# Full-width one-hots in place of column tiles in the first level of an edge sum

## The chip, the cores and the metric

The kernel runs on one core of a Trainium2 chip. The metric is the device time of one execution in microseconds; nine runs of the kernel before are given by their median. TensorE (PE) multiplies matrices, VectorE (DVE), ScalarE (ACT) and GpSimd (POOL) work on tiles in SBUF and PSUM, SyncE (SP) issues transfers. Each engine takes its instructions in a fixed order, and waits between engines are semaphores.

## What is computed

A graph with 12,500 nodes of 64 features and 400,000 edges, sorted by destination, passes two layers.

```python
def _L0_gnn_ref(x, edge_attr, ...):
    x_t = _mlp2(x, W1n, b1n, W2n, b2n)
    e_t = _mlp2(edge_attr, W1e, b1e, W2e, b2e)
    msgs = x_t[src] * e_t * dp_scale
    aggregated = jax.ops.segment_sum(msgs, dst, num_segments=num_nodes)
    out = x + aggregated * res_w
    ...                       # layernorm with gamma, beta
def _L1_gnn_ref(x, edge_index, W, b):
    ...                       # K = 2 hops: h = segment_sum(edge_weight * h[col], row)
    return h @ W.T + b
x = _layernorm(x + _L0_gnn_ref(x, ...))
x = _layernorm(x + _L1_gnn_ref(x, ...))
```

The change touches the `segment_sum` of the first layer: sums of message rows over edges with the same destination.

## The kernel before

A step `q` of 261 handles 12 chunks (`QC`) of 128 edges. Four consecutive superchunks of three chunks (`SCC`) make a step, and the destinations of a superchunk lie within 32 consecutive nodes (`REL`). Steps run from the last edge to the first, and a step is spread over four passes of the main loop, so that four steps are in flight:

- `hidden` (L624 to L638): the first layer of the edge network, two f32 matmuls on row tiles, then ACT and DVE.
- `message` (L648 to L659), in two halves: second layer on PE, and on DVE the product with the gathered rows `xg`, into one of three message tiles `msg` of 65 columns (the last is 1, for the degree).
- `level1` (L674 to L693): DVE builds the one-hot `oh` (128 edges x 12 chunks x 32 columns) of each edge's node within its superchunk's 32. PE multiplies each chunk's one-hot (128x32, the stationary side) with its messages (128x65) and adds the three chunks of superchunk `s` into partitions 32`s` to 32`s`+31 of a PSUM bank `pl`; each superchunk has its own column tile of PE. ACT copies the bank to `tot` (L693). The 128 rows of `tot` are sums for the four windows of 32 nodes.
- `level2` (L703, L713): a second one-hot puts these rows into their window of 128 nodes in a PSUM `ring`; it runs one pass later.

GpSimd gathers the rows `xg` (L592), 12 indirect transfers a step, paced by marks on PE's matmuls. When a group of nodes is complete, `nodes` normalises it.

Between these units the main loop interleaves two generators: `adjacency` (L859 to L944), which builds a dense table of edge counts from one-hots on DVE (L910, a pool `ohp` of 11 buffers), matmuls (L920) and copies on ACT (L935), and `hop1` (L1097 to L1251), which multiplies the table with node features (L1117, L1129), copies the result (L1169) and turns it (L1246, f32, 128x128 weights, 64 columns). From about 5780 us only the second hop and the output remain (L1221, L1232, L1479, L1594).

A scheduler with a model of engine times puts the instructions into each engine's order; the units of the main loop have high priority. A tile in a pool with n buffers can be written again when the n-th last use has ended. The one-hot `oh` of level 1 lives in `edgep` with two buffers; PSUM has seven banks for all users beside the ring.

Of the kernel before, what the change touches and what calls it, by code (L numbers as in the profile page):

```python
# [11 lines left out]
F32 = mybir.dt.float32  # L12
# [9 lines left out]
P = 128  # L22
# [10 lines left out]
SCC = 3  # L33
QC = 4 * SCC
# [6 lines left out]
REL = 32  # L41
# [157 lines left out]
def tile_fast(  # L199
# [42 lines left out]
    nc = tc.nc  # L242
# [34 lines left out]
    with tc.tile_pool(name="srch", bufs=2) as srch, tc.tile_pool(  # L277
        name="srch1", bufs=1
# [125 lines left out]
        iota_f = const.tile([P, 4 * P], F32, name="iota_f")  # L404
# [51 lines left out]
        with tc.tile_pool(name="tmp1", bufs=1) as t1:  # L456
            r = t1.tile([1, D], F32, name="b2r")
            nc.sync.dma_start(r, b2e[None, :])
            for k in range(3):
                h = t1.tile([1, D], BF16, name=f"b2h{k}")  # L460
                nc.vector.tensor_copy(h, r)
                if k < 2:
                    r2 = t1.tile([1, D], F32, name=f"b2r{k}")
                    nc.vector.tensor_sub(r2, r, h)
                    r = r2
# [46 lines left out]

    edgep = main.enter_context(tc.tile_pool(name="edgep", bufs=2))
    msgp = main.enter_context(tc.tile_pool(name="msgp", bufs=1))
    hopp = main.enter_context(tc.tile_pool(name="hopp", bufs=3))
    hevp = main.enter_context(tc.tile_pool(name="hevp", bufs=2))
    lnp = main.enter_context(tc.tile_pool(name="lnp", bufs=1))
    counts = ExitStack()
    slotp = counts.enter_context(tc.tile_pool(name="slotp", bufs=1))
    slotq = counts.enter_context(tc.tile_pool(name="slotq", bufs=2))  # L520
    ohp = counts.enter_context(tc.tile_pool(name="ohp", bufs=11))
    kohp = counts.enter_context(tc.tile_pool(name="kohp", bufs=10))
    stgp = counts.enter_context(tc.tile_pool(name="stgp", bufs=3))
    psR = main.enter_context(tc.tile_pool(name="psR", bufs=1, space=PSUM))
# [2 lines left out]
    def bank(shape, name):  # L527

        n = math.prod(shape[1:])
        t = banks.tile([P, 512], F32, name=name, tag="bank")[:, :n]  # L530
        if len(shape) == 3:
            t = t.rearrange("p (a b) -> p a b", b=shape[2])
        elif len(shape) == 4:
            t = t.rearrange("p (a b c) -> p a b c", b=shape[2], c=shape[3])
        return t
# [4 lines left out]
    for i in range(3):  # L540
        m = msgp.tile([P, QC, D + 1], F32, name=f"msg{i}")
# [127 lines left out]
    def level1(q):  # L669
        def f():  # L670
            _, rel = seg[q // SEGQ]
            c0 = (q % SEGQ) * QC
            oh = edgep.tile([P, QC, REL], F32, name="oh1")
            nc.vector.tensor_tensor(  # L674
                oh,
                iota_f[:, None, :REL].to_broadcast([P, QC, REL]),
                rel[:, c0 : c0 + QC, None].to_broadcast([P, QC, REL]),
                op=ALU.is_equal,
            )
            pl = bank([P, D + 1], "pl")  # L680
            m = msgs[q % 3]
            for s in range(4):
                for c in range(SCC):
                    nc.tensor.matmul(  # L684
                        pl[REL * s : REL * (s + 1), :],
                        oh[:, s * SCC + c, :],
                        m[:, s * SCC + c, :],
                        start=(c == 0),
                        stop=(c == SCC - 1),
                        tile_position=(0, REL * s),  # L690
                    )
            tot = edgep.tile([P, D + 1], F32, name="tot")
            nc.scalar.copy(tot, pl)  # L693
            tots[q] = tot

        return f
# [634 lines left out]
    for t in range(NQ + 3):  # L1331
# [23 lines left out]
        for u in range(parts * len(units)):  # L1355
# [5 lines left out]
            while a_live and a_spent < a_goal:  # L1361
                c = next(a_gen, None)
# [5 lines left out]
            while h_live and h_budget > 0:  # L1368
                try:
                    c = next(h_gen)  # L1370
# [301 lines left out]
    for c in range(NSC):  # L1672
        if c + 1 < NSC:
            tiles[c + 1] = [load_dense(*d, c + 1) for d in dense]
        w = min(SC, PITCH - c * SC)
# [45 lines left out]
        for j in range(max(0, min(-(-w // P), W0 - wi0))):  # L1721
            m = min(P, w - j * P)
# [5 lines left out]
                start=False,  # L1728
                stop=False,
                skip_group_check=True,  # L1730
            )
        for j in range(max(0, min(-(-w // P), W0 - wi0))):
            m = min(P, w - j * P)
# [5 lines left out]
                start=False,  # L1739
                stop=False,  # L1740
                skip_group_check=True,
                tile_position=(0, D * h),
# [572 lines left out]
def build(nc, fast, general, params, out, **kw):  # L2315
    with tile.TileContext(nc, schedule_with_timeline_sim=True) as tc, ExitStack() as ctx:
        fp = ctx.enter_context(tc.tile_pool(name="flag", bufs=1))
        flag = fp.tile([1, 1], I32, name="flag")
        tile_fast(tc, flag, *fast, *params, out, **kw)
        again = nc.values_load(flag, min_val=0, max_val=1)  # L2320
        with tc.If(again > 0):
            tile_general(
                tc, *general, *params, out.rearrange("(p j) d -> p j d", j=NJ)
            )
# [27 lines left out]
```

## Time and profile before

| quantity | value |
|---|---|
| median of 9 runs | 6575.74 us (6550.13 to 6584.31) |
| the profiled execution, its own time | 6566.46 us |
| its span from first to last instruction | 6564.7 us |
| mean granted PE clock, share of full | 0.801 |
| PE busy | 5072.8 us, 77% of the span |
| GpSimd busy | 3744.3 us, 57% |
| DVE busy | 3321.8 us, 51% |
| ACT busy | 2272.1 us, 35% |
| level 1's one-hots on DVE (L674) | 261, 145.7 us, 558 ns each |
| level 1's copies on ACT (L693) | 261, 56.2 us, 215 ns each |

The profile is of one execution. Busy time counts instructions, not waits. The end of a matmul is modelled, so a matmul record tells when it was started and not surely when its result was there. An f32 matmul leaves two records. The granted clock of PE switches between 1.0 and 0.5. A wait is put down to the instruction whose semaphore ended it; "remote" or "unknown queue" stands where no instruction's end fits, and "issue" where the profile shows no wait.

### The profile page before, as it was taken

The numbers are of one execution on the slowest core, as the hardware profiler recorded it, in microseconds if no ns is written. First come the engines' busy times: TensorE is split into PE (matmuls) and PEld (weight loads), VectorE is DVE, ScalarE is ACT, GpSimd is POOL, SyncE is SP. The second block draws the span as 40 slices with busy tenths as digits, with TensorE's granted clock in tenths as the row PEclk, the third lists the DMA queues.
The fourth block names the chain that finished last, engine by engine and source line by source line (L and its number), as shares of the span: only waits on it lengthen the run. The fifth ranks groups of instructions, "written<-read, shape, count | busy, mean of one in ns | idle before, by whom it ended". The sixth has DMA issues, their size and how long they took to land. (4 is left out here: it accounts for less than half of the span.)

```text
span 6564.7 us, 94126 instructions
## 1 busy us (share of the span) xinstructions
PE 5072.8 (77%) x31344; PEld 2865.0 (44%) x31344; DVE 3321.8 (51%) x11086; ACT 2272.1 (35%) x7868; POOL 3744.3 (57%) x3607
## 2 busy tenths in 40 slices
PE   4666788888888788876777678867866786589998
PEld 2333344544444444443444444434434443344444
DVE  5667565555455555555555555555656664330003
ACT  2667565444333333333333333223322111220002
POOL 5666455556555555555444555555665553448886
PEclk6777788888887787777777678878877786599999
DMA  3655454544444354423333243323322223269998
GB/s 105 144 128 120 108 124 111 113 112 108 102 106 100 76 114 99 96 62 85 87 92 89 55 101 88 87 53 91 88 56 58 56 55 98 75 166 212 210 201 216
DMA packets 1254835, 696.95 MB, mean 106 GB/s; under 512 B 593468, under 2 KB 1188144, under 8 KB 1253312
## 3 DMA queue, kind: packets, MB, share of 16 engines
q1 hardware_dynamic: 1104032, 566.91, 34.0%
q0 software_dynamic: 150304, 123.92, 11.2%
q8 instruction: 248, 4.06, 0.3%
q14 instruction: 251, 2.06, 0.1%
HBM read 494.67 MB, written 195.83 MB: 105 GB/s over the span
## 5 line engine op out<-in xcount | busy, mean ns | idle before, releaser
L592 POOL DMA_INDIRECT xg<-xt_tab,si x3125 | 3080.8, 986 | 2549.8 <-PE pa L920 768.0
L935 ACT ACTIVATE stage<-pa 128x391 fp8e4<-128x391 f32 x3077 | 1507.6, 513 | 1563.5 <-PE pa L920 1109.4
L910 DVE TENSOR_SCALAR oh<-iota_b,colT 128x391 bf16<-128x391 bf16 x5556 | 1620.6, 333 | 737.9 <-PE pa L920 466.3
L920 PE MATMUL pa<-oh,koh 128*128 128x391 bf16 (+2 forms) x6054 | 1412.6, 406 | 276.5 <-issue 135.7
L920 PEld LDWEIGHTS <-koh 128*128 128x128 bf16 (+2 forms) x6054 | 627.6, 154 | 780.3 <-issue 526.8
L1117 PE MATMUL hacc_p<-at,gp 128*128 128x512 fp8e4 (+1 forms) x2425 | 768.4, 454 | 87.3 <-DMA at<-adj 38.0
L624 PE MATMUL pw<-eat,w1ab 64*128 64x384 f32 x1044 | 511.0, 763 | 285.3 <-ACT tot L693 209.5
L935 ACT ACTIVATION_READ_ACCUMULATOR stage<-pa 128x1 f32 x3077 | 673.4, 219 | 0.0
L674 DVE TENSOR_TENSOR oh<-iota_f,rel 128x384 f32<-128x384 f32 x261 | 145.7, 558 | 999.1 <-remote 739.9
L713 PE MATMUL ring<-tot,oh 128*128 128x65 f32 x1096 | 260.1, 384 | 405.0 <-ACT tot L693 340.6
L1492 POOL DMA_INDIRECT hop_tab<-tot,first x317 | 493.7, 1558 | 101.0 <-issue 95.7
L650 PEld LDWEIGHTS pe<-w,z 128*128 128x128 f32 x3132 | 475.1, 213 | 106.9 <-issue 86.2
L650 PE MATMUL pe<-w,z 128*128 128x128 f32 x3132 | 485.5, 296 | 0.0
L1117 PEld LDWEIGHTS <-gp 128*128 128x128 bf16 x2425 | 262.6, 115 | 477.0 <-issue 289.3
L713 PEld LDWEIGHTS ring<-tot,oh 128*128 128x128 f32 x1096 | 220.9, 283 | 556.4 <-ACT tot L693 389.9
L693 ACT COPY tot<-pl 128x65 f32<-128x65 f32 x261 | 56.2, 215 | 1145.4 <-remote 794.0
L659 DVE TENSOR_TENSOR msg<-pe,xg 128x384 f32<-128x384 f32 x522 | 288.0, 552 | 322.0 <-PE pe L650 245.6
L1221 PE MATMUL acc<-at,gp 128*128 128x512 fp8e4 (+1 forms) x2000 | 446.3, 376 | 0.0
L1129 PE MATMUL hacc_p<-at,gp 128*64 128x512 fp8e4 (+1 forms) x2425 | 386.9, 401 | 11.9 <-issue 11.3
L859 DVE TENSOR_TENSOR koh<-iota_k,keyT 128x512 bf16<-128x512 bf16 (+3 forms) x920 | 384.9, 420 | 0.0
L634 ACT ACTIVATE z<-pw,b1s 128x384 f32<-128x384 f32 x522 | 290.9, 599 | 215.4 <-PE pw L624 105.7
L1246 PEld LDWEIGHTS pc<-twoid,hev 128*128 128x128 f32 x1764 | 332.5, 274 | 75.2 <-issue 40.7
(218 smaller groups left out, 4381.1 us busy)
## 6 DMA issues: line engine op xcount, KB each, us to landing
adj<-stage SPq DMA_DIRECT2D x390, 391.0 KB
at<-adj SPq DMA_DIRECT2D x97, 896.0 KB
at<-adj SPq DMA_DIRECT2D x168, 512.0 KB
eat<-in_eaq_dram SPq DMA_DIRECT2D x261, 192.0 KB
xg<-xt_tab,si POOLq DMA_INDIRECT x3125
at<-adj SPq DMA_DIRECT2D x96, 256.0 KB
at<-adj SPq DMA_DIRECT2D x24, 832.0 KB
at<-adj SPq DMA_DIRECT2D x24, 768.0 KB
```

Of the source, the lines that this page charges most:

```text
L592: got = nc.gpsimd.indirect_dma_start(out=xg[:, i, :], out_offset=None, in_=xt_tab, in_offset=bass.IndirectOffsetOnAxis(ap=si[:, c : c + 1] ...
L624: nc.tensor.matmul(pws[h], w1ab[rows, h, :], ea_q[rows], start=True, stop=True, tile_position=(D * h, 0),)
L650: ended = nc.tensor.matmul(pe[:, :, c, :], z[:, h, c * P : (c + 1) * P], w2, start=False, stop=(c == SCC - 1),)
L713: nc.tensor.matmul(ring[:, w % RING, :], oh[:, (w - lo) * P : (w - lo + 1) * P], tot, start=False, stop=False, skip_group_check=True,)
L859: nc.vector.tensor_tensor(t[:, :, :n], iota_8[:, :, :n] if w == 8 else iota_k[:, : w * FA, :n], keyT[:, None, j0 : j0 + n].to_broadcast([P ...
L910: nc.vector.tensor_scalar(oh, iota_b, colT[:, i % P : i % P + 1], None, op0=ALU.is_equal)
L920: ended = nc.tensor.matmul(to, key, oh, start=(j == 0), stop=(j == caps[g] - 1), tile_position=(0, r0),)
L935: nc.scalar.activation(stage[:, u, :], pa, AF.Identity, saturate=True, accum_out=sums[:, u : u + 1],)
L1117: nc.tensor.matmul(acc[:, :w], gp[:kk, lo + i, 0:2, :].rearrange("p t d -> p (t d)"), t[:kk, i, :w], start=start, stop=False, skip_group_c ...
L1129: nc.tensor.matmul(acc[D * h : D * (h + 1), :w], gp[:kk, lo + i, 2, :], t[:kk, i, :w], start=False, stop=False, skip_group_check=True, til ...
L1221: nc.tensor.matmul(acc[:, :w], gp[:kk, wi, 0:2, :].rearrange("p t d -> p (t d)"), t[:kk, wi - lo, :w], start=first and n == 0, stop=False, ...
L1492: nc.gpsimd.indirect_dma_start(out=hop_tab[(q * QC + i) % HT], out_offset=bass.IndirectOffsetOnAxis(ap=first[:, q - Q0, i : i + 1], axis=0 ...
```

## The change

Level 1's one-hot of a chunk becomes 128 columns wide. Only the 32 columns of its superchunk are written; the others are zero. The tile `ohw`, one buffer, is set to zero once before the loop. It holds for each superchunk three blocks of 128 columns, of which the one-hot fills the first 32, and 32 columns of padding behind them. The weights of a chunk are a window of 128 columns that begins 32`s` columns before its own block, so that the one-hot lies at columns 32`s` to 32`s`+31 of the window and the rest of it falls on zeros. All twelve chunks add into the whole bank `pl` as one group (`start` at the first, `stop` at the last), at tile position (0, 0). The one-hot on DVE compares the same 384 elements and writes them in runs of 32. The pool `ohp` has ten buffers instead of eleven.

```diff
+    OHW = 128
+    OHC = SCC * OHW // REL
+    OHP = SCC * OHW + REL
+    ohw = msgp.tile([P, 4 * OHP], F32, name="ohw")
+    nc.vector.memset(ohw, 0.0)
+    oh_own = (
+        ohw.rearrange("p (s k) -> p s k", k=OHP)[:, :, : SCC * OHW]
+        .rearrange("p s (c w) -> p s c w", w=OHW)[:, :, :, :REL]
+    )
...
-    ohp = counts.enter_context(tc.tile_pool(name="ohp", bufs=11))
+    ohp = counts.enter_context(tc.tile_pool(name="ohp", bufs=10))
...
-            oh = edgep.tile([P, QC, REL], F32, name="oh1")
+            four = [P, 4, SCC, REL]
             nc.vector.tensor_tensor(
-                oh,
-                iota_f[:, None, :REL].to_broadcast([P, QC, REL]),
-                rel[:, c0 : c0 + QC, None].to_broadcast([P, QC, REL]),
+                oh_own,
+                iota_f[:, None, None, :REL].to_broadcast(four),
+                rel[:, c0 : c0 + QC]
+                .rearrange("p (s c) -> p s c", c=SCC)[:, :, :, None]
+                .to_broadcast(four),
                 op=ALU.is_equal,
             )
             pl = bank([P, D + 1], "pl")
             m = msgs[q % 3]
-            for s in range(4):
-                for c in range(SCC):
-                    nc.tensor.matmul(
-                        pl[REL * s : REL * (s + 1), :],
-                        oh[:, s * SCC + c, :],
-                        m[:, s * SCC + c, :],
-                        start=(c == 0),
-                        stop=(c == SCC - 1),
-                        tile_position=(0, REL * s),
-                    )
+            for c in range(QC):
+                s, r = c // SCC, OHW * (c * REL // (SCC * OHW))
+                o = s * OHP - REL * s + r + OHW * (c % SCC)
+                nc.tensor.matmul(
+                    pl[r : r + OHW, :],
+                    ohw[:, o : o + OHW],
+                    m[:, c, :],
+                    start=(c % OHC == 0),
+                    stop=(c % OHC == OHC - 1),
+                    tile_position=(0, r),
+                )
```

## The prediction

> **What bounds the kernel now.** I read the page's head first, then the groups of instructions by line and shape, then the waits, and last the timeline around single level-1 sums.
>
> ```profile
> span 6564.7 us, 94126 instructions
> PE 5072.8 (77%) x31344; PEld 2865.0 (44%) x31344; DVE 3321.8 (51%) x11086; ACT 2272.1 (35%) x7868; POOL 3744.3 (57%) x3607
> ```
>
> The last 785 us (second hop, from 5780 us) hold no level 1. The 261 level-1 sums lie between 196.4 and 5780.7 us, 21.48 us a step, and there TensorE (PE) is idle for 1344 us, 5.1 us a step. No engine is full: PE stays first, but something makes it wait.
>
> ```profile
> L1246 PE MATMUL pc<-twoid,hev 128*128 128x64 f32 x1746 | 344.4, 361 | 22.4 <-issue 10.1 <-ACT hev L1169 9.9 <-ACT stage L935 2.1
> ...
> L684 PE MATMUL pl<-msg,oh 128*32 128x65 f32 x6264 | 294.2, 230 | 90.2 <-issue 54.3 <-DVE msg L659 24.3 <-DVE chk L961 7.3
> ```
>
> ```profile
> ACT tot L693 <- remote: 794.0, 143, 11.7
> ...
> DVE oh L674 <- remote: 739.9, 142, 8.4
> ...
> PE ring L713 <- ACT tot L693: 340.6, 88, 10.6
> ...
> PE pw L624 <- ACT tot L693: 209.5, 60, 7.1
> ```
>
> The first fence holds groups by line and shape: busy us, mean ns of one, idle us before it and what ended that. The second holds waits: total us, times, longest. Each f32 matmul leaves two records, so a level-1 sum (12 matmuls) has 24. They look cheap: 294.2/261 = 1.13 us a sum. But the copy out of the sum's bank (L693), which waits for the last of them alone, waits 794 us for a signal that the profile can't match to a finished instruction ("remote"), and PE itself then loses 340.6 + 209.5 = 550 us to that copy. The timeline shows one case.
>
> ```profile
> 5117.74 1.97 PE L1246 MATMUL pc<-twoid,hev 128*128 128x64 f32 x8
> ...
> 5126.71 1.00 PE L1246 MATMUL pc<-twoid,hev 128*128 128x64 f32 x8
> ...
> 5128.80 0.68 PE L684 MATMUL pl<-msg,oh 128*32 128x65 f32 x12
> ...
> 5130.93 0.91 PE L624 MATMUL pw<-eat,w1ab 64*128 64x384 f32 x2
> ...
> 5138.36 0.56 DVE L674 TENSOR_TENSOR oh<-iota_f,rel 128x384 f32<-128x384 f32 x1 [4.57 <-remote]
> 5138.36 0.21 ACT L693 COPY tot<-pl 128x65 f32<-128x65 f32 x1 [11.69 <-remote]
> ...
> 5138.63 1.65 PE L624 MATMUL pw<-eat,w1ab 64*128 64x384 f32 x2 [6.80 <-ACT tot L693]
> ```
>
> The sum's records end at 5129.48, PE goes on to 5131.84, and the copy starts only at 5138.36, with VectorE's (DVE's) L674, which waits for the same sum. All three engines stand. Over all 261 sums the copy starts a mean 4.9 us after the last L684 record starts (1271 us in all), and PE is idle for 718 us of these windows. No other f32 group does this: where a message product (L659) waits for its L650 matmuls at full clock, it starts a median 0.31 us after the last record in 105 cases with no level 1 in the 7 us before, and 1.9 us in the 24 with one. At half clock level 1's own copies start a median 0.41 us after. So 128x32 f32 tiles in four column groups at full clock signal late, and what follows them in PE's order signals late with them.
>
> **The change, part by part.**
>
> *Late signals go.* The new matmuls have the shape of L713 and L1246 (128x128 weights, f32, 64 or 65 columns), which signal on time. The idle at stake is 718 us. Not all is won: behind the stall waits the next thing, the one-hots of the adjacency (L910) on a DVE that is busy 3281 of the first 6500 us, 12.6 us a step. Comparing steps within each stretch of 500 us, a step is 0.46 to 0.97 us longer per us that its copy is late in eight stretches of twelve and hardly longer in three, but groups of four steps show no slope at all (0 +- 0.2), so the bounds are 0 and 718; I take three quarters, because the chain of waits in its last 900 us before the second hop puts 19.1% into such unmatched signals: **-540 us**.
>
> *PE work.* 24 records a sum stay, but each loads 128 columns. The two L1246 lines price it: (1.00-0.22)/7 = 0.111 us a record at full clock, (1.97-0.42)/7 = 0.22 at half (0.22 and 0.42 are the tail of a last record). That makes 24 x 0.111 = 2.7 us or 5.3 us a sum against 1.13. With the granted clock at 0.78 over the stage, 44% of it is at half; if that falls to 30%, a sum takes 3.4 us, +2.3, in all **+594 us of PE time**. It lies partly in the 2.4 us of idle a step that remain (1344-718 over 261). The lower bound is 0, the upper 261 x (5.3-1.13) = 1088; I let 0.6 through, since a step lengthens by about 0.5 us per us of full-clock PE work in it when groups of four steps are compared: **+356 us**.
>
> *Clock.* 188 of the 245 half-clock stretches, 1877 of their 2478 us, begin in a stall of more than 1.5 us or within 4.5 us of one. PE is busy 81% of half-clock time; if half of these stretches stay at full clock, 380 us of PE time go. The bounds are 0 and 760; a third of 380 for what reaches the end: **-130 us**. The Trainium skill ("TensorE: Matmul & The Clock Gate", The HAM clock gate) states that an idle window of about 3.4 us halves the clock; PE stands from 5131.84 to 5138.63 us above and the clock is at half from 5133.3 us, in line with that rule, and by it all 1877 us would go.
>
> *The one-hot.* DVE still compares 384 elements (558 ns, L674), now written in runs of 32 at a stride of 128: between nothing and twice 558 ns a step, on an engine with 9 us of slack a step; nothing. The tile is one buffer instead of two, so the one-hot of step k waits for the sum of k-1, not k-2. In the built order it moves from 47 DVE instructions ahead of its message product to 8 behind (a step has 41). The sum stands 81 matmuls behind the message, more than a step (72), so nothing waits for the one-hot; L910 one-hots are queued behind it in 228 of 261 cases, as in 200 before, and PE waits for these. That exposure is the present one (739.9 us at L674) and shrinks with the signal's delay. One setting to zero of 1664 columns, before the loop, is below 4 us (512 take 0.95 us, L1642).
>
> *Ten buffers for L910 instead of eleven.* PE's waits for it are 22.1 us, those of the weight loads 31.9; bounds 0 and +54, taken as nothing.
>
> *Order.* PE's queue keeps its sequence; 6 sums instead of 43 have foreign matmuls between their own, and 13.6 instead of 12.0 matmuls stand between a sum and its level 2. Both are worth little.
>
> Sum: -540 + 356 - 130 = **-314 us**, on the profiled run's 6566.46 us (span 6564.7) 6252; the median of the nine runs lies 9 us above that run: **6260 us**.
>
> **Rivals.**
>
> *PE becomes the bound (slower).* The packing into column tiles hid weight loading, and giving it up costs more than the stall did. For it: the four-step comparison, in which late copies cost nothing because DVE and GpSimd were behind anyway. Then +356 to +594 with nothing back: 6930 to 7170; with a small part back, from 6600. It decides once less than 1.4 us of idle a sum (0.6 x 2.3) is recovered. Against it: 19.1% of the chain. The Trainium skill speaks for this rival ("TensorEngine Tiling (Array Packing)", When to Use Tiling): it advises column tiles at up to four times the speed where the stationary side is 32 wide. This case's trace agrees as far as records go (12 in 0.68 us), not for the signal.
>
> *The stall stays.* If it came from the f32 sum over twelve chunks or from its copy, it would outlive the tiles, and PE's price comes on top: 6930 to 7170. Against it: the timely L650 and L1246.
>
> *More than the sum.* PE stays at full clock and nothing takes the stall's place. The 28 steps whose copy is 1 to 3 us late take 18.98 us at a clock of 0.90, against 21.4 over all; with the new price nearly the same as their delay, 261 x 2.4 = 626 us go: 5950. GpSimd would not stop it: 12 gathers x (0.99 + 0.30) us = 15.4 us a step.
>
> *Cancelled.* Both terms meet within 13 us.
>
> **How the numbers follow.** Forecast 0.55, PE-bound 0.17, more 0.17, stall stays 0.06, cancelled 0.05. The likeliest case's own range is 6050 to 6480. Taking in half of "more" and the milder part of PE-bound gives 5880 to 6750. Faster by over 0.2% (13 us, what a measurement can tell from no change): 0.55 + 0.17 = 0.72; within: 0.05; slower: 0.23.
>
> **What would show it.** Right: the copy after level 1 starts within 0.5 us of the last record; "remote" waits at the copy and the one-hot fall from 794 and 740 us to below 150; level 1's 6264 records have shape 128x128 and take 0.11 us each at full clock; granted clock above 0.83 in the first 5700 us; level 1 near 900 us of PE time. Wrong: late copies remain (stall stays), or PE is above 85% busy with no idle before L713 and the time is above 6600 (PE-bound).

## The result: 3.4% faster where it was measured first, for another reason than predicted

The changed kernel takes 6354.79 us (median of 10 runs, 6327.73 to 6367.96) against 6570.86 us (31 runs, 6550.13 to 6597.65): a ratio of 0.9665 [0.9649, 0.968], 216 us less. Its profiled execution took 6333.93 us. The page's head and, from the groups by line and shape, level 1's matmul and one-hot:

```profile
span 6332.2 us, 93866 instructions
PE 5338.0 (84%) x31344; PEld 3308.9 (52%) x31344; DVE 3321.3 (52%) x11087; ACT 2258.1 (36%) x7868; POOL 3742.4 (59%) x3607
...
L698 PE MATMUL pl<-msg,ohw 128*128 128x65 f32 x6264 | 785.6, 283 | 36.9 <-issue 25.0 <-ACT stage L949 7.3 <-DVE msg L670 4.2
...
L685 DVE TENSOR_TENSOR ohw<-iota_f,rel 128x384 f32<-128x384 f32 x261 | 145.7, 558 | 964.4 <-remote 504.9 <-PE pa L934 303.6 <-PE pl L698 56.3
```

Level 1's matmuls (L684 before, now L698) cost 491 us more of PE time, the one-hot (now L685) the same 558 ns. The waits (total us, times, longest) show the copy at L707, before L693:

```profile
ACT tot L707 <- remote: 553.6, 103, 8.7
...
DVE ohw L685 <- remote: 504.9, 102, 8.4
...
PE ring L727 <- ACT tot L707: 244.0, 87, 6.1
...
PE pw L635 <- ACT tot L707: 90.7, 51, 3.7
```

These fell from 794.0, 739.9, 340.6 and 209.5 us. They did not vanish. From the last record of a sum to its copy a mean of 3.6 us passes, before 4.9; from the *first* record to the copy 6.5 us where the sum's first and last record are at full clock (231 sums), and before just as long (226 sums). The delay stayed; the sum's own records grew there from a median 0.74 to 2.62 us and fill more of it. The accounts of the stretch from the first to the last level-1 record, which holds the whole gain (the tail behind it takes 784 us in both):

| level-1 stretch | before | after | difference |
|---|---|---|---|
| length, us | 5584 | 5354 | -230 |
| PE idle | 1344 | 848 | -496 |
| PE busy | 4241 | 4506 | +265 |
| of it level 1's records | 294 | 786 | +491 |
| granted clock | 0.781 | 0.830 | |

PE does 491 us more in level 1 and 226 us less elsewhere (the same instructions at a better clock), and is idle for 496 us less. So the added work and the idle time that went cancel, and the gain is the better clock: of the other PE work, counted by the clock at each record's start, 1862 us were at half clock before and 1429 us after. The signals' delay is what has to be explained, and a timeline of the kernel after shows what goes with it (start and duration in us, engine, line, operation; in brackets the idle time before it and what ended that):

```profile
1729.22 0.94 POOL L603 DMA_INDIRECT xg<-xt_tab,si  x1 [2.52 <-PE pe L661]
1730.47 0.95 POOL L603 DMA_INDIRECT xg<-xt_tab,si  x1 [0.30 <-issue]
...
1732.25 2.79 PE L698 MATMUL pl<-msg,ohw 128*128 128x65 f32 x24
...
1735.46 0.94 POOL L603 DMA_INDIRECT xg<-xt_tab,si  x1 [0.30 <-issue]
...
1736.71 0.95 POOL L603 DMA_INDIRECT xg<-xt_tab,si  x1 [0.30 <-issue]
...
1739.34 0.56 DVE L685 TENSOR_TENSOR ohw<-iota_f,rel 128x384 f32<-128x384 f32 x1 [6.29 <-PE pa L934]
1739.34 0.21 ACT L707 COPY tot<-pl 128x65 f32<-128x65 f32 x1 [5.70 <-PE pa L934]
...
1739.71 1.00 POOL L603 DMA_INDIRECT xg<-xt_tab,si  x1 [2.05 <-PE pa L934]
```

GpSimd gathers (L603, before L592) without a pause over the sum and 2.6 us beyond its last record. The gather at 1736.71 is the last; it ends at 1737.66, and 1.68 us later DVE, ACT and then GpSimd itself get their signals from PE. That is the clue. The experiments look for the reason in level 1's own matmuls first.

### The profile page after: what moved, and what is told of

Read it like the earlier page. It is cut to its first block, busy times and chain, and to the rows that moved or that the text cites. A ratio compares the mean times of both kernels' runs of the same rounds, so it can differ in the third digit from the quotient of the medians.

```text
span 6332.2 us, 93866 instructions
## 1 busy us (share of the span) xinstructions
PE 5338.0 (84%) x31344; PEld 3308.9 (52%) x31344; DVE 3321.3 (52%) x11087; ACT 2258.1 (36%) x7868; POOL 3742.4 (59%) x3607
## 4 chain that ended last, share of the span: by engine, by line
PE 71%; another core or an unknown queue 11%; ACT 6%; DVE 4%; issue 4%; DMA 1%; SPq 0%; POOL 0%; DVEq 0%; POOLq 0%; ACTq 0%
PE pa L934 16%; PE hacc_p L1131 10%; PE pl L698 8%; PE acc L1235 6%; PE pw L635 6%; PE pe L661 6%; PE hacc_p L1143 5%; PE pc L1260 4%; ACT stage L949 4%; PE acc L1246 3%; PE ring L727 3%; PE pe L659 2%; DVE oh L924 1%; PE pk L1092 1%
## 5 line engine op out<-in xcount | busy, mean ns | idle before, releaser
L603 POOL DMA_INDIRECT xg<-xt_tab,si x3125 | 3077.6, 985 | 2305.2 <-issue 681.2
L934 PE MATMUL pa<-oh,koh 128*128 128x391 bf16 (+2 forms) x6054 | 1381.3, 394 | 199.6 <-issue 88.7
L698 PEld LDWEIGHTS pl<-msg,ohw 128*128 128x128 f32 x6264 | 767.3, 200 | 104.2 <-issue 57.1
L698 PE MATMUL pl<-msg,ohw 128*128 128x65 f32 x6264 | 785.6, 283 | 36.9 <-issue 25.0
L1131 PE MATMUL hacc_p<-at,gp 128*128 128x512 fp8e4 (+1 forms) x2425 | 725.4, 433 | 82.6 <-DMA at<-adj 36.8
L949 ACT ACTIVATION_READ_ACCUMULATOR stage<-pa 128x1 f32 x3077 | 686.1, 223 | 0.0
L685 DVE TENSOR_TENSOR ohw<-iota_f,rel 128x384 f32<-128x384 f32 x261 | 145.7, 558 | 964.4 <-remote 504.9
L635 PE MATMUL pw<-eat,w1ab 64*128 64x384 f32 x1044 | 450.5, 692 | 103.1 <-ACT tot L707 90.7
L707 ACT COPY tot<-pl 128x65 f32<-128x65 f32 x261 | 55.9, 214 | 1221.2 <-remote 553.6
L727 PE MATMUL ring<-tot,oh 128*128 128x65 f32 x1096 | 229.3, 347 | 269.4 <-ACT tot L707 244.0
L727 PEld LDWEIGHTS ring<-tot,oh 128*128 128x128 f32 x1096 | 194.1, 249 | 394.1 <-ACT tot L707 282.5
```

The lines of the kernel that those rows point to most:

```text
L603: got = nc.gpsimd.indirect_dma_start(out=xg[:, i, :], out_offset=None, in_=xt_tab, in_offset=bass.IndirectOffsetOnAxis(ap=si[:, c : c + 1] ...
L635: nc.tensor.matmul(pws[h], w1ab[rows, h, :], ea_q[rows], start=True, stop=True, tile_position=(D * h, 0),)
L698: nc.tensor.matmul(pl[r : r + OHW, :], ohw[:, o : o + OHW], m[:, c, :], start=(c % OHC == 0), stop=(c % OHC == OHC - 1), tile_position=(0, r),
L727: nc.tensor.matmul(ring[:, w % RING, :], oh[:, (w - lo) * P : (w - lo + 1) * P], tot, start=False, stop=False, skip_group_check=True,)
L934: ended = nc.tensor.matmul(to, key, oh, start=(j == 0), stop=(j == caps[g] - 1), tile_position=(0, r0),)
L949: nc.scalar.activation(stage[:, u, :], pa, AF.Identity, saturate=True, accum_out=sums[:, u : u + 1],)
```

## Experiments

The expectations were written in the order of the runs. "Late" below means a copy of level 1 that starts over 2 us after the last record of its sum; "on time", within 0.6 us. The chip's number is given, for it turned out to matter. Each chip was used at one time alone, so what differs between chips may also be the state that a chip was in then.

### Four column tiles again, or two, or filler work, or BF16 (chip 1)

```diff
-    OHW = 128
+    OHW = 32        # first run; 64 in the second
```
```diff
+            fill = bank([P, FB], "fill")       # third run, on top of the first
+            for i in range(12):
+                nc.tensor.matmul(fill, identb, iota_b, start=True, stop=True)
```
```diff
-    ohw = msgp.tile([P, 4 * OHP], F32, name="ohw")     # fourth run, with OHW = 128
+    ohw = msgp.tile([P, 4 * OHP], BF16, name="ohw")
-        m = msgp.tile([P, QC, D + 1], F32, name=f"msg{i}")
+        m = msgp.tile([P, QC, D + 1], BF16, name=f"msg{i}")
```

The first, with four column tiles, undoes the width alone:

> The changed kernel with the four column tiles of 32 back and all else kept: the one-hot tile ohw in one buffer, ten buffers for the adjacency one-hots, the code of the loop. If the full width makes the gain, the time is that of the kernel before (6570 us, within 0.5%) and level 1's copies on ACT start a mean 4.9 us after the last record again. If instead the tile, the pools or the order they lead to make it, the time stays near 6355 us.

The second has two column tiles of 64:

> Two column tiles of 64 columns, two superchunks each. If column tiles delay the signal, two of them delay it as four do and the time is near 6570 us. If what counts is that PE is occupied by the sum while the signal is awaited, the 24 records take about half as long as at full width and the time lies between, near 6460 us.

The third puts 12 matmuls, whose result nobody reads, behind each sum of the first:

> Column tiles of 32 as in the first, and behind each level-1 sum 12 further bf16 matmuls of 391 columns (2.0 us at full clock) into a bank that nobody reads. If the gain comes from PE being kept busy and its clock high during the late signal, whatever work does it, the time falls from that of the first towards 6355 us, by 100 us or more, with the granted clock from 0.80 to above 0.83. If full-width weights matter for themselves, the added 261 x 2.0 = 520 us of PE time costs something: 6600 to 6900 us.

The fourth keeps 128 columns and makes both operands BF16:

> The changed kernel with level 1's one-hots and the messages in bf16 (the low bits of the messages are left out): 12 records a sum instead of 24, each about half as long. If the late signal belongs to f32 matmuls of 65 columns, the copies start within 0.5 us of the last record, PE saves about 500 us, and the time is 5950 to 6200 us. If it belongs to the place in the step and not to the type, the copies still come 3 us or more late, and the time is 6250 to 6450 us.

| | us | ratio to before on this chip | PE busy / idle in the stretch |
|---|---|---|---|
| before | 5046.31 | | |
| 32 columns | 5043.47 | 0.9995 [0.9983, 1.0006] | 3620 / 491 |
| 64 columns | 5055.80 | 1.0014 [1.0002, 1.0027] | 3642 / 487 |
| 32 and filler | 5185.21 | 1.0271 [1.0250, 1.0293] | 3959 / 294 |
| 128, BF16 | 5043.76 | 0.9994 [0.9981, 1.0006] | 3508 / 601 |

These runs did not tell the theories apart: the kernel before itself takes 5046 us on this chip, not 6571, and there is no delay here to be won back. With 32 columns the copies that wait start 0.25 to 0.41 us after the last record from 1000 us on (148 sums). So four column groups of 128x32 f32 matmuls do signal on time. What follows: the delay belongs to something that differs between chips, and where it is absent 2 us of PE work a step cost 2.7%.

### Level 1's forms by themselves (chip 6)

A bench runs 12 f32 matmuls with 128 columns, with four column tiles in two orders, with 64, 65 and 128 moving columns, three matmuls alone, and 12 in BF16, each between bf16 matmuls and followed by a copy, first with GpSimd quiet and then beside 160 gathers:

```python
heat(26)      # bf16 matmuls ahead
case()        # one of the forms, its copy on ACT behind it
tail(14)      # bf16 matmuls behind
```

> A bench: level-1 sums by themselves, each six times between 26 bf16 matmuls before and 14 behind, first without and then with a stream of gathers on GpSimd; nothing of the reference is computed. Kinds: f32 128 columns wide with 65 moving columns, 12 chunks (the change); four tiles of 32, three chunks of a tile in a row (before); the same with tiles taking turns; f32 with 64 moving columns; three chunks only; 128 moving columns; bf16. If column tiles delay the signal, only the two tiled kinds have copies later than 0.5 us after the last record. If f32 with 65 columns does, the first kind has them too and bf16 has not. If none has, the delay needs something else of the kernel around it.

Every form signals on time, with gathers or without: the copy starts 0.29 to 0.51 us after the last record in all 84 groups. The 24 records take 2.51 us with 128 columns and 0.74 us in column tiles in the order of the kernel before (0.33 us where the tiles take turns). But the kernel before took 5071.65 us on this chip: it too is one where nothing is late, so the bench bears on the price of the records and not on the delay.

### Both kernels on one chip without the delay (chip 12)

> The changed kernel as it stands, beside the kernel before on one chip, whichever that is. In the runs on the chip with number 1 the kernel before took 5046 us and its level-1 copies followed the last record of the sum within 0.5 us, so there is no late signal there to win back. Theory now (the gain is idle of the late signal that is filled, and it belongs to the chip or session in which before took 6571 us): where before takes about 5050 us the change wins nothing and pays for 261 x (2.6 - 0.7) = 480 us of added PE work, part of it hidden: ratio 0.998 to 1.03. Where before takes about 6570 us: ratio near 0.967. Rival (the gain comes with the shape of the matmuls wherever it runs): ratio near 0.967 on any chip.

> The kernel before, for its trace on the same chip as the changed kernel. If it takes about 5050 us here: the copy starts within 0.5 us of the last record of the sum, remote waits at the copy and the one-hot are below 100 us, and PE is busy 85 to 90%. If it takes about 6570 us: 794 and 740 us of remote waits, as in the profile before. The trace should show which durations of instructions, if any, differ between the two conditions; theory: none on any engine, only the time from record to signal; rival: the gathers, the clock or an engine's instructions are slower there and the late signal only follows.

The changed kernel takes 5174.36 us against 5069.49: a ratio of 1.0214 [1.0195, 1.0232], slower. The head of the page, level 1's records and the copy's wait, of the kernel before here:

```profile
span 5066.5 us, 94126 instructions
PE 4407.2 (87%) x31344; PEld 2578.4 (51%) x31344; DVE 3274.8 (65%) x11086; ACT 2269.2 (45%) x7868; POOL 3784.3 (75%) x3607
...
L684 PE MATMUL pl<-msg,oh 128*32 128x65 f32 x6264 | 279.7, 229 | 121.8 <-DVE msg L659 116.3 <-ACT stage L935 4.0 <-DVE top L958 1.0
...
L693 ACT COPY tot<-pl 128x65 f32<-128x65 f32 x261 | 60.9, 233 | 240.1 <-PE pl L684 208.7 <-PE pa L920 26.4 <-issue 4.1
```

and of the changed kernel:

```profile
L698 PE MATMUL pl<-msg,ohw 128*128 128x65 f32 x6264 | 751.4, 277 | 7.7 <-DVE msg L670 5.5 <-ACT stage L949 1.7
...
L707 ACT COPY tot<-pl 128x65 f32<-128x65 f32 x261 | 56.2, 215 | 582.2 <-PE pl L698 574.0 <-issue 5.4 <-PE pa L934 2.5
```

No "remote" is left at the copy: 151 of 163 waits before and 244 of 248 after end with a matmul of the sum. The same instructions stand in the same order as in the profile before and take the same time: a gather 997 ns here and 986 there, an adjacency one-hot 336 and 333, a level-1 record 229 and 230. Only the time from PE's records to its signals differs, and with it the clock (0.912 and 0.801). The step is 15.92 us long, and GpSimd's twelve gathers, which start 1.249 us apart when none waits, take 15.0 of it. That suggests why 472 us more of level 1 on PE cost only 105 us here: they lie beside the gathers.

### Half of the gathers (chip 3)

```diff
-    GATE = 8
+    GATE = 4
...
-        xg = xgs[q] = xgp.tile([P, QC, D], F32, name="xg")
+        xg = xgs[q] = xgp.tile([P, QC // 2, D], F32, name="xg")
...
+            if i % 2:
+                yield
+                continue
...
-                xgs[q][:, k * h : k * (h + 1), :],
+                xgs[q][:, :k, :],
```

`GATE`, the distance in gathers to the mark that paces them, is halved with their number.

> The kernel before with half of GpSimd's gathers of the first layer left out (six a step; the second half of a step is multiplied with the rows of the first half, so the output is not the reference's). Theory (where the copy is on time, the gathers pace the step: 12 x 1.249 = 15.0 us of 15.9 us, and PE's work lies beside them): the step falls to PE's own time and waits, 13 to 14.5 us, and the kernel to 4450 to 4800 us. Rival (PE, with 87% busy, paces the step already): within 1.5% of the kernel before, 5000 to 5070 us. Should this chip show the late copies of the first profile (kernel before near 6570 us), half the gathers should change little there: 6400 to 6600.

> The changed kernel with the same half of the gathers left out. Theory (the gathers hide most of level 1's added PE work, of which only 105 of 470 us came through with all gathers): without them the added PE work shows nearly in full, 250 to 450 us above the kernel before with half the gathers. Rival (PE paces in both, and its added work costs a fifth wherever it lies): 80 to 150 us above. On a chip with late copies: below the kernel before with half the gathers, by about 3%.

The kernel before took 5060.78 us on this chip; with half the gathers it takes 4636.07 (0.9153 [0.912, 0.9186]), and the changed one 5018.32 (0.9912 [0.9881, 0.9943]). Both theories held. The gathers pace a step where signals are on time; without half of them PE is the bound (93 and 95% busy in the stretch), and the change costs 382 us for 490 us of added level-1 records, 0.78 us a us instead of 0.22.

### Twice the filler, on a chip with late signals (chip 11)

```diff
-            for i in range(12):
+            for i in range(24):
                 nc.tensor.matmul(fill, identb, iota_b, start=True, stop=True)
```

> Column tiles of 32 as in the kernel before, and behind each level-1 sum 24 instead of 12 matmuls whose result nobody reads (4 us of TensorE work a step at full clock; twelve, 2 us, took 5185 us against 5046). Where the copies are on time (kernel before near 5050 us): the first 2 us were mostly hidden beside the gathers, which take 15.0 us a step, and TensorE was then idle for only 294 us of 261 steps, so theory expects the second 2 us to come through for 60 to 100%: 5490 to 5700 us. Rival (each 2 us costs the same 140 us): 5325. Where the copies are late (kernel before near 6570 us): theory (the delay is a fixed time from the sum's first record, which any TensorE work can fill) expects 6300 to 6600 us, not slower; rival (the delay follows the last work queued): above 6900.

This chip is one of the others: the kernel before takes 6570.05 us on it. With 32 columns and 4 us of filler a step the kernel takes 6681.61 us, 1.0163 [1.0087, 1.0239]. Neither expectation holds, the theory misses by 80 us. The copy's wait:

```profile
ACT tot L710 <- remote: 940.4, 197, 15.5
...
ACT tot L710 <- PE fill L708: 250.0, 43, 9.6
```

The filler did not shorten the delay (a mean of 5.4 us from the last record, and, counted as above, 6.4 from the first), and PE's idle time in the stretch is 841 us, as after the change (848). So each of the two kernels fills about 500 us of the 1344 idle us, the change with its 491 us of level 1 alone, and the filler beyond that made the kernel longer, although the mean clock was 0.906. Half of this filler was not run on such a chip, so whether other work of the change's size gains as much there is not shown.

### Four forms of level 1 in one kernel (chip 0), and with half the gathers (chip 10)

```diff
+            kind = q % 4
+            n = (12, 6, 3, 12)[kind]
+            for c in range(n):
+                s = c // SCC
+                o = s * OHP - REL * s + OHW * (c % SCC)
+                w, v = ohw[:, o : o + OHW], m[:, c, :]
+                if kind == 3:
+                    w = w.bitcast(BF16).rearrange("p (k t) -> p k t", t=2)[:, :, 1]
+                    v = v.bitcast(BF16).rearrange("p (k t) -> p k t", t=2)[:, :, 1]
+                nc.tensor.matmul(pl, w, v, start=(c == 0), stop=(c == n - 1))
```

> The changed kernel with four forms of the level-1 group, by the step's number modulo four: 12 f32 matmuls as in the change, 6, 3 (the other chunks left out of the sum), and 12 matmuls that read the upper halves of the same f32 words as BF16 (low bits left out). On a chip with late copies (kernel before near 6570 us) the trace tells what the delay hangs on. Theory A (a long run of f32 passes: 24 records): the copy follows the first record by about 6.2 us in the first form, by under 2 us in the third and in the BF16 form. Theory B (a fixed delay of whatever group comes in this place, with any number of passes): near 6 us in all four. Theory C (a price per f32 pass, about 6.2/24 = 0.26 us each): 6.2, 3.2, 1.6 us and under 2 us in BF16. On a chip without late copies (kernel before near 5060 us): within 3 us of the first record in all forms, and 5040 to 5120 us, nothing told apart.

5079.02 us beside 5056.13 us of the kernel before: a chip without the delay, nothing told apart, as expected for that case.

> Half of the gathers left out, as in the two runs before, and level 1 in the four forms of the last run (12, 6 and 3 f32 matmuls of 128 columns and 12 that read the upper halves as BF16; parts of the sums are left out). Without late copies (kernel before near 5060 us): level 1 is then 385 us of TensorE records by the last run, against 257 with column tiles (4636 us) and 747 with 12 f32 matmuls of 128 columns (5018 us). Theory (the price of the change is its TensorE time, (5018-4636)/(747-257) = 0.78 us a us): 4636 + 0.78 x 128 = 4740, +-60. Rival (the one buffer of the one-hot, its strided writes or the full bank cost it): 4950 to 5050. On a chip with late copies (kernel before near 6570 us): first record to copy as in the last run's expectation, 6.2 us in all forms (a fixed delay), or 6.2, 3.2, 1.6 and below 2 us (a price per f32 pass), or 6.2 us in the first form alone (a long run of passes).

Here the kernel before takes 6562.67 us, so this is a chip with late signals, and yet this kernel takes 4813.72 us: 0.7335 [0.7314, 0.7356]. Its head, its gathers and its copy:

```profile
PE 4389.8 (91%) x28614; PEld 2667.1 (55%) x28614; DVE 3235.4 (67%) x11087; ACT 2252.8 (47%) x7868; POOL 2272.2 (47%) x2045
...
L606 POOL DMA_INDIRECT xg<-xt_tab,si x1563 | 1607.4, 1028 | 2254.3 <-PE pa L938 1682.0 <-PE pe L664 303.1 <-issue 204.9
...
L711 ACT COPY tot<-pl 128x65 f32<-128x65 f32 x261 | 58.9, 226 | 343.0 <-PE pl L707 239.7 <-PE pa L938 56.0 <-issue 12.9
```

The "remote" is nearly gone here too (12.8 us at the copy, in 6 waits). All three theories about level 1's form fall. Where the sum's first and last record are at full clock and the copy waits, the medians are:

| form | sums | first to last record, us | first record to copy, us | last record to copy, us |
|---|---|---|---|---|
| 12 f32, as in the change | 61 | 2.62 | 2.93 | 0.31 |
| 6 f32 | 47 | 1.28 | 1.59 | 0.31 |
| 3 f32 | 49 | 0.61 | 0.93 | 0.37 |
| 12 BF16 | 49 | 0.38 | 1.56 | 1.16 |

The first row is the change's own form, word for word. It signals 0.31 us after its last record; in the profile after it took a median of 4.1 us (229 sums). What differs is half of the gathers, and that the other three steps of four are lighter; no run took the two apart on such a chip. The trace does in part: at the last record of 52 of these 61 sums no gather was under way. The BF16 row, 1.16 us against 0.23 on chip 0, and single copies up to 4.1 us late show that the delay is not quite gone. The time of this run does not test the 0.78 us a us, which was meant for a chip without the delay.

## On the chips with the delay, PE's signals are late beside GpSimd's gathers

With that, the trace of the kernel before reads differently. These are GpSimd's lines of the timeline around the sum that the prediction showed, whose copy starts at 5138.36:

```profile
5131.82 0.96 POOL L592 DMA_INDIRECT xg<-xt_tab,si  x1 [0.30 <-issue]
...
5133.08 0.94 POOL L592 DMA_INDIRECT xg<-xt_tab,si  x1 [0.30 <-issue]
...
5134.33 0.94 POOL L592 DMA_INDIRECT xg<-xt_tab,si  x1 [0.30 <-issue]
5135.57 0.94 POOL L592 DMA_INDIRECT xg<-xt_tab,si  x1 [0.30 <-issue]
```

The chain of gathers ends at 5136.51, 1.85 us before the copy. Counted over the whole trace, three views agree:

- *Release.* 207 copies start over 2.5 us after the last record. In 41 a gather is running at that moment; of the other 166, 151 start 1.0 to 2.25 us after the end of GpSimd's last instruction. Of all moments without a running GpSimd instruction, from the first sum to the last copy, only 20% lie so. After a gather that 2 us of quiet follow, its last packet ends a median 1.16 us behind its record; so most of these copies start within a microsecond after GpSimd's transfers are through. (The Trainium skill, "Perfetto Trace Analysis", DMA Instruction — SWDGE (GPSIMD), states that the profiled end of such an instruction is that of generating its descriptors, not of moving the data; the 1.16 us agree.) A moment 1.5 us earlier has no gather begun in the 1.2 us before it in only 43 of the 207, the moment of the copy in 159.
- *Every signal of PE, not level 1's alone.* Waits for adjacency matmuls (L935 for L920, bf16) with no level 1 in the 7 us before, at full clock: with GpSimd busy under 20% of the last 3 us, none of 85 comes over 2 us late; with over 60%, 16 of 84. For L659 behind L650: none of 50, and 5 of 25. Behind L1246, which the prediction called timely: with level 1 near and GpSimd busy, 24 of 25. Signals from ACT are on time beside busy gathers: DVE's L638 starts 33 ns after ACT's L634 in all 25 cases. The trace's own records of the signals say the same: while the gathers last, 3488 of PE's 7073 come late, without a PE record that ended up to 25 ns before (or a series of signals under 60 ns apart that began so), and on chip 12 5 of 8238; of DVE's 5864 none is late in this way, of ACT's 2843 three. (DVE and ACT should have left 9190 and 4486; on chip 12 99% are there. With over a third of these records missing, a releaser that the profile names on these chips can be the wrong one.)
- *Place among the gathers.* How many waiting copies at full clock are late depends on what GpSimd does at the sum's last record. A row here is a run of gathers of which each starts within 0.4 us of the last one's end:

| late copies | no gather under way | first to third gather of a row | fourth or later |
|---|---|---|---|
| kernel before | 6 of 11 | 76 of 93 | 114 of 115 |
| kernel after | 1 of 14 | 32 of 48 | 158 of 167 |
| filler, chip 11 | 3 of 8 | 76 of 84 | 140 of 144 |
| half the gathers and four forms, chip 10 | 1 of 95 | 7 of 86 | 7 of 25 |
| kernel before, chip 12 | 0 of 2 | 0 of 9 | 0 of 133 |

Where the last row had ended 2 us or more before, none of 28 copies in the first four traces is late. On chip 10 a row is 1.8 gathers long, against 4.2 in the kernel before. That copies beside a fourth gather are late less often there is not explained by the row alone.

*The chips without the delay.* On chip 12 GpSimd is busier (75%, not 57%), and of 130 waiting copies at full clock with gathers before them 127 are on time. In the profile before, 2 of 205 such copies are, and 184 are late. So gathers alone do not make signals late: it takes a chip of the one kind as well.

GpSimd is itself paced by marks on PE's matmuls, at a distance of eight gathers; its longest wait in the kernel before is for such a matmul (L920):

```profile
L592 POOL DMA_INDIRECT xg<-xt_tab,si x3125 | 3080.8, 986 | 2549.8 <-PE pa L920 768.0 <-issue 686.3 <-PE pe L650 603.7
```

On the chips with the delay the two seem to hold each other up: the gathers go on until their marks run out, PE's signals come when the transfers have ended, among them the marks, and both start again. That would explain why the time from a sum's first record to its copy hardly depends on what PE does: 6.5 us with 24 short records, 6.5 with 24 long ones, 6.4 with filler behind them (means), and 3.8 to 3.9 gathers begun meanwhile in all three. That the gathers hold the signals back is read from these counts and from the run with half of them; no run took away the gathers alone on such a chip. What makes chips differ stays open, and so does what is late: as a matmul's end is modelled, it can be the signal or the result itself. PE's signals come late together: at 1739.31 us in the trace after, five come 34 ns apart.

## Why the prediction was right in time and wrong in its reason

*Late signals go (-540).* This step failed. It took from the trace that "128x32 f32 tiles in four column groups at full clock signal late" and that the new shape would "signal on time". Copies were to start within 0.5 us and the remote waits to fall below 150 us; they start after 3.6 us, and 553.6 and 504.9 us remain. Column tiles are on time in the traces of four chips (1, 3, 12 and, in the bench, 6), and 128 columns are late on the first. The evidence was a comparison in which two things changed: the 105 timely waits without level 1 that it counted hold 50 with GpSimd quiet, none of them late, and 25 with GpSimd busy, five late. Level 1 stands where gathers run: 205 of its 251 waiting sums were at full clock with GpSimd busy before the last record. The timeline shown left out GpSimd's row, and the rival "the stall stays" was closest to what happened to the delay. The *size* came out near by luck: 496 us of idle went, because added matmuls fill a delay that stayed.

*PE work (+594, of it 0.6).* A record takes 0.11 us at full clock as said, and level 1 rose by 491 us. The share that comes through is a property of the stage, not of the matmul: 0.22 beside all gathers and 0.78 beside half of them where signals are on time; on the first chip all 491 us came through and took the place of the 496 us of idle. So these two terms, -540 and +356, together -184, measured -496 and +491, together -5.

*Clock (-130).* This term was too small, and it holds nearly the whole gain: 226 us of other PE work went. The clock rose from 0.781 to 0.830, and half-clock time between the first and the last level-1 record fell from 2447 to 1825 us. That the sum of -314 lay near the -216 measured is luck: two terms that should have left 184 us left 5, and the third was 96 us short. The rule of the Trainium skill cited there ("TensorE: Matmul & The Clock Gate", The HAM clock gate), by which all 1877 us of half clock next to stalls would go, asked for the stalls to go first, and they did not. Nor is the case shown in line with that rule, though the prediction reads it so: PE had stood for 1.5 us when the half clock began at 5133.3, and only 43 of the 242 half-clock stretches between the first and the last level-1 record begin after 3.4 us or more without a PE record.

*One-hot, buffers, order.* The one-hot's 558 ns and its single buffer cost nothing that shows: with 32 columns and the new buffering the time is that of the kernel before (0.9995), so the three edits together are worth nothing there.

*PE becomes the bound.* This rival is what the change does on the one chip where PE signals on time and both kernels ran unaltered: 2.1% slower. The rule named for it (the Trainium skill, "TensorEngine Tiling (Array Packing)", When to Use Tiling: use column tiles where the stationary side is 32 wide) holds in the bench, 0.74 us against 2.51 us a group. A forecast of 6930 us was wrong for it because it charged the full work on top of the stalls.

No kernel with the whole result was shown to be faster than the one before on both kinds of chips. On chips with the delay a pause in the gathers while a sum's signal is due might gain far more than the change; that was not tried.

## What to carry to other kernels

When a wait is released by nothing the profile can name, line its end up with every engine, also those that neither kernel nor wait connects with it, and compare cases that differ in one thing. Work put into a stall is free only while the stall is there: know which resource then paces the step before calling it a gain. If two kernels differ by some per cent on one chip, run both on another before keeping the faster.

## What the hardware showed that was not expected

The kernel before takes 5046 to 5072 us on five chips (0, 1, 3, 6, 12) and 6563 and 6570 us on two (10, 11), as in the runs it was first measured in; on each chip the runs of one kernel agree within 0.8%. Instructions take the same time on both kinds (a gather 986 and 997 ns). On the kind with the delay PE's signals come late while GpSimd's gathers are under way, up to 9.2 us in the trace before. The change measured -3.4% on a chip of one kind and +2.1% on a chip of the other.
